# Order of the first key and value products in a two-way cross attention: the next sequence's keys placed before this sequence's values

## The chip, the cores and the metric

The kernel runs on one core of one Trainium2 chip. Its time is device microseconds for one execution. The five engines are named as the profile names them: PE (matmul; PEld its weight loads), DVE (vector), ACT (scalar), POOL (GpSimd) and SP (which issues most DMAs). All data are float32.

## The reference, cut to what matters

There are 16 sequences of 100 rows of `x` (640 wide), each with an encoder context of 722 rows (384 wide). The last 4 context rows are the tokens. Eight heads of 80.

```python
query = hidden_states @ Wq
keyt = enc @ Wk          # 718 keys
valt = enc @ Wv
hs = _mha(query, keyt, valt)
ca_q1 = jnp.einsum('btc,th->bch', ca, Wq_ca)[:, indices, :]
ca_hs1 = _mha(ca_q1, residual, residual)
ca_q2 = ca_hs1 @ Wq
ca_hs2 = _mha(ca_q2, ca @ Wk_ca, ca @ Wv_ca)
out = (hs + ca_hs2) @ Wout + b_out + residual
```

## The kernel before, in words

One loop `for b in range(B)` goes over the sequences, and from there on the order in which the program is written is the order of each engine's queue; each engine works through its own queue in that order and waits only on semaphores.

The middle sequences, b = 1 to 14, run like this:

- *Scores.* `scores` (products L609) fills PSUM with the scores of sequence b in three groups. Groups 0 and 2 lie in two double banks from the pool `pair`; group 1 lies in two banks of the pool `psumk` and two of `psum1`. ACT copies them to `st` (L665 for the double banks, L659 for the others). DVE takes the maximum over them (`most`, L1270 and L1282).
- *Tokens' product.* `now.softmax2()` (L1287) multiplies the exponentials `e1` with the tokens' table `y_sb` on PE: 64 small matmuls (L825) into `z_ps`, one bank of `psum1`. DVE reads it (L834, L836).
- *Keys of b + 1 and values of b.* Both are 3 by 2 blocks of products of the context with a weight. They are done with 15 products instead of 18, by sums of context pieces and of weights made before (a fast scheme for small matrix products). POOL makes the sums of the context, 13 additions (`enc_sums`, L500), one sequence ahead; other pieces are used as loaded. The plans `V_PLAN` and `K_PLAN` list the 15 products in order, each with the bank it is summed in (A to E) and the block that the running sum goes to. `go(n)` of a `Values` or `Keys` object takes the next n products: the matmuls (V: L434, two of them, one per half of the keys; keys: L465, two), and behind each the transfer of the running sum: for a block's first arrival a copy on ACT (L407, into `vs` or `kT`), for a later one an addition on DVE (L405). A bank's next product must wait until the running sum has been read. `both(n)` takes n of V's and then n of the keys'.
- *Banks.* V's A and B are a pair of double banks, which held the scores of group 2. V's C, D and E take two banks of `psum1` each. The keys' A and B are the two banks of `psumk`, which held scores of group 1; their C, D and E are one bank of `psum1` each.
- *Softmax.* While these products run, DVE and ACT turn the maximum into `top.over` (`top.go`, L700 to L730; ACT's part is `spread`, L722), DVE subtracts it from `st` (L1258), and ACT takes exponentials (L1266).
- *POOL* works through the next sequence's first token scores (`scores1`, L798 and L805; its first instruction waits for the maximum over this sequence's scores), small pieces of the second softmax (L864, L878), the bias on rows of `x` (L932, only in sequences that load such rows), and the tokens' values (`values2`, L892, L899).
- After the products come the fifth chunk of the next keys (`last_keys`, L559), in some sequences the output projection (L1050) and the next queries (L535), and then the attention's sum `a_ps` (L1455).

The order around the change: `softmax2` (L1287), `second.scores1` (POOL, L1345), `top.go(3)` (DVE, L1346), `both(3)` (L1347), `scores2` (L1348).

Of the kernel before, what the change touches and what calls it, by code (L numbers as in the profile page):

```python
# [126 lines left out]
def kernel(  # L127
# [80 lines left out]
    def enc_tile(name):  # L208

        return inp.tile([P, NF, KT], F32, tag="enc", name=name)  # L210
# [14 lines left out]
    def load_rest(b, enc):  # L225
        if b == 1:
            room = hsT_tile("rest_1").rearrange("p c s -> p (c s)")
            rest = room[:, : len(A_REST) * KT].rearrange("p (i k) -> p i k", k=KT)
        else:
            rest = rest_tile(f"rest_{b}")  # L230
        for (u, c), i in A_REST.items():
            nc.sync.dma_start(
                out=rest[:, i], in_=enct[b][:, c, u * (KT - 1) : u * (KT - 1) + KT]
            )
        return enc[0], rest
# [348 lines left out]
    def last_keys(b, enc):  # L584
        banks = pair(f"kT_ps_{b}")
        return chunk_keys(
            HC - 1,
            [banks[:, k] for k in range(2)],
            [wk4[:, c] for c in range(CC)],
            enc,  # L590
        )
# [140 lines left out]
    def load_m(b):  # L732
        if b < 2:
            return lambda c: m_sb[c][:, b * HT : (b + 1) * HT]
        mb = small.tile([P, HC, HT], F32, tag="mb", name=f"mb_{b}", bufs=2)
        nc.sync.dma_start(
            out=mb, in_=m_d[:, :, b * HT : (b + 1) * HT].rearrange("c p n -> p c n")
        )
        return lambda c: mb[:, c]
# [496 lines left out]
    for b in range(B):  # L1236
# [5 lines left out]
        def loads():  # L1242

            if b == 0:
                nc.sync.dma_start(
                    out=wout_sb, in_=wout.rearrange("(c p) n -> p c n", p=P)
                )
            if b + 2 >= B:
                return None, None
            x_next = xT_at[0] if b % 2 else load_x(p + 1)  # L1250
            xT_at[0] = x_next
            return Second(b + 2, x_next), load_enc(b + 2)
# [4 lines left out]
        def subtract(i):  # L1257
            return nc.vector.tensor_tensor(  # L1258
                st[i],
                st[i],  # L1260
                top.over[:KN].unsqueeze(1).to_broadcast([KN, 2, ROWS]),
                ALU.subtract,
            )

        def exponential(i):
            nc.scalar.activation(st[i], st[i], AF.Exp, scale=SCALE)  # L1266
# [26 lines left out]
        if b + 1 < B:  # L1293
            kk = Keys(b + 1, enc)
# [32 lines left out]
        elif b + 1 < B:  # L1327
            vv = Values(b, e_in)

            def both(n):  # L1330
                vv.go(n)
                kk.go(n)

            forms = [wout_sb[:, 2 * i : 2 * i + 2, k * (H // 2) : (k + 1) * (H // 2)]
                     for i in range(2) for k in range(2)]
            if b == 2:
                for o, left, right in (
                    (forms[1], forms[1], forms[0]),
                    (wout2[:, 0], forms[3], forms[1]),
                    (wout2[:, 1], forms[2], wout2[:, 0]),  # L1340
                ):
                    nc.gpsimd.tensor_tensor(o, left, right, ALU.subtract)
            elif last.b - 1 in PAIRS:
                nc.gpsimd.tensor_tensor(wout2[:, 0], wout2[:, 0], forms[0], ALU.add)
            second.scores1(seen, range(T - 1))  # L1345
            top.go(3)  # L1346
            both(3)  # L1347
            now.scores2(nc.gpsimd)  # L1348
            second.scores1(None, range(T - 1, T))
            if b == 1:  # L1350
                now.load()
            last.load()
            top.go(1)
            if b > 1:
                last.place()
            now.exponentials2()
            both(2)
            both(2)
            top.go()
            both(1)  # L1360
            now.softmax3()
            if b == 1:
                nc.gpsimd.tensor_tensor(last.hs[:S], last.hs[:S], last.hs2, ALU.add)
            if last.b in PAIRS:
                last.sums()
            now.values2()
            vv.go(2)
            kk.go(1)
            subtract(0)
            exponential(0)  # L1370
            vv.go(1)
            subtract(1)
            vv.go(1)
            kk.go(2)
            exponential(1)
            vv.go(1)
            kk.go(2)
            both(1)
            both(1)
            if b == 1:  # L1380
                for f in list(wv_there):
                    nc.scalar.copy(wv_sb[:, W_AT[f]], wv_there.pop(f))
            second.load()
            if b == 1:
                nc.gpsimd.dma_start(out=bias, in_=bout[0].partition_broadcast(P))
            second_next, enc_next = loads()
            if b + 2 < B:
                m_next = load_m(b + 2)
            subtract(2)
            exponential(2)  # L1390
            last_keys(b + 1, enc)
            if b + 2 < B:
                enc_next = load_rest(b + 2, enc_next)
            if b == 1:
                last.transpose()
            if last.b in PAIRS:
                second.softmax1(3)
                last.project_pair()
                if last.b == max(PAIRS):
                    nc.sync.dma_start(  # L1400
                        out=forms[1],
                        in_=wout[: 2 * P, H // 2 :].rearrange("(c p) n -> p c n", p=P),
                    )
            second.softmax1()
        else:
            room = enc_tile("spare").rearrange("p f k -> p (f k)")
            spare.extend(room[:, i * H : (i + 1) * H] for i in range(2))
            last.transpose()
            vv = Values(b, e_in)
            last.load()  # L1410
            mine.load()
            top.go(3)
            vv.go(3)
            last.project_few(len(OC) - 2)
            now.scores2(nc.gpsimd)
            now.exponentials2()
            top.go(1)
            vv.go(2)
            top.go()
            vv.go(3)  # L1420
            now.softmax3()
            now.values2()
            vv.go(2)
            subtract(0)
            exponential(0)
            vv.go(5)
            for i in (1, 2):
                subtract(i)
                exponential(i)
            last.project()  # L1430
# [108 lines left out]
```

## Time and profile before

| what | time |
|---|---|
| median of 3 runs | 927.17 us (927.08 to 928.4) |
| the profiled execution | 927.45 us, span 925.7 us |
| PE busy | 916.2 us, 99% of the span |
| POOL, DVE busy | 684.5 us, 680.8 us (74% each) |
| ACT busy | 433.6 us (47%) |
| V's products into A (L434) | 352 matmul rows of 437 ns |
| keys' products into A (L465) | 360 matmul rows of 367 ns |
| waits of PE for ACT at V's first product | 2.6 us, 9 times |

A row of a timeline gives start and length in us (starts from the beginning of the span), engine, line, operation, tile written <- tiles read, shapes and count of instructions merged into it; in brackets stands how long the engine sat idle before it and what ended that. The matmuls are pipelined, so the rows of consecutive groups overlap by a few tenths; the distance between the starts of two groups is the better measure of what a group costs. A row of waits reads: engine, tile and line that waited, <- engine, tile and line it waited for: us in total, times, longest. A row of the chain of waits gives shares of the span.

### The profile page before, as it was taken

The page shows a single profiled execution, that of the slowest core. Times are in us where ns is not written, and L with a number is a line of the kernel's source. Part 1 is how long each engine was busy: PE and PEld are TensorE (multiplying, and loading weights), DVE is VectorE, ACT ScalarE, POOL GpSimd, SP SyncE. Part 2 cuts the span into 40 slices and gives each one's busy share as a digit, 9 for nine tenths or more (in the row PEclk, how much of TensorE's full clock was granted, in tenths as well). Part 3 has the DMA queues.
Part 4 walks back from the last instruction along what each step waited for, and adds up shares of the span by engine and source line. Part 5 has one row for each costly group of instructions (what it writes and reads, how often), then busy time and mean ns, then how long its engine had stood idle before and what let it go on. Part 6 is the DMA issues. An engine that isn't in the chain of part 4 may idle for free.

```text
span 925.7 us, 26204 instructions
## 1 busy us (share of the span) xinstructions
PE 916.2 (99%) x11290; PEld 772.5 (83%) x11290; DVE 680.8 (74%) x1085; ACT 433.6 (47%) x836; POOL 684.5 (74%) x647
## 2 busy tenths in 40 slices
PE   9999999999999999999999999999999999999998
PEld 6988889787797979888798787988879787797866
DVE  3459795989739896785967869579883898838883
ACT  2235543737336463552636426264641737427341
POOL 5749999787937878497884968757996579956723
PEclk9999999999999999999999999999999999999999
DMA  8822023050300304031030411205031050310201
GB/s 263 273 76 78 25 60 83 5 152 2 107 27 17 112 6 127 3 98 58 23 111 3 110 46 30 76 2 154 3 91 42 2 154 2 104 45 2 82 19 41
DMA packets 49675, 62.85 MB, mean 68 GB/s; under 512 B 14072, under 2 KB 38200, under 8 KB 49560
## 3 DMA queue, kind: packets, MB, share of 16 engines
q1 hardware_dynamic: 45512, 51.49, 18.6%
q0 software_dynamic: 3024, 8.53, 3.1%
q8 instruction: 89, 1.46, 0.7%
q10 hardware_dynamic: 1024, 1.15, 0.4%
q14 instruction: 26, 0.21, 0.1%
HBM read 55.59 MB, written 5.57 MB: 66 GB/s over the span
## 4 chain that ended last, share of the span: by engine, by line
PE 97%; ACT 1%; DMA 0%; issue 0%; DVE 0%; POOL 0%; ACTq 0%; POOLq 0%
PE s_ps L609 12%; PE a_ps L1455 12%; PE v_psA L434 11%; PE v_psB L434 9%; PE k_psA L465 8%; PE kT_ps L559 8%; PE q_ps L535 7%; PE k_psB L465 7%; PE o_ps L1050 5%; PE v_psC L434 3%; PE k_psC L465 3%; PE v_ps L375 2%; PE v_psD L434 2%; PE v_psE L434 2%; PE y_ps L773 1%; PE k_psE L465 1%
## 5 line engine op out<-in xcount | busy, mean ns | idle before, releaser
L798 POOL TENSOR_TENSOR e<-ca,g 100x800 f32<-100x800 f32 x64 | 97.9, 1540 | 124.7 <-PE v_psD L434 99.8
L500 POOL TENSOR_TENSOR enc<-enc 128x240 f32<-128x240 f32 x135 | 109.8, 822 | 18.3 <-DMA enc<-in_enct 11.2
L1258 DVE TENSOR_TENSOR st<-st,over 120x1600 f32<-120x1600 f32 x48 | 117.4, 2448 | 0.0
L1455 PEld LDWEIGHTS a_ps<-vs,st 120*36 120x36 f32 (+3 forms) x3072 | 109.2, 125 | 4.9 <-issue 4.8
L434 PE MATMUL v_psA<-wv_sb,enc 128*120 128x320 f32 x352 | 110.6, 437 | 2.5 <-ACT st L665 2.3
L1455 PE MATMUL a_ps<-vs,st 120*36 120x81 f32 (+3 forms) x3072 | 112.0, 233 | 0.0
L899 POOL TENSOR_TENSOR hs<-hs,hs 100x640 f32<-100x640 f32 x48 | 99.0, 2063 | 3.8
L805 POOL TENSOR_TENSOR e<-e,e 100x800 f32<-100x800 f32 x48 | 93.6, 1950 | 3.8
L892 POOL TENSOR_TENSOR hs<-vb,p 100x640 f32<-100x640 f32 x64 | 91.3, 1436 | 3.9 <-DMA vb<-va_d 0.9
L434 PE MATMUL v_psB<-wv_sb,enc 128*120 128x320 f32 x296 | 91.9, 433 | 0.0
L1266 ACT ACTIVATE st<-st 120x1600 f32<-120x1600 f32 x48 | 73.9, 1539 | 33.4 <-DVE st L1258 33.4
L465 PE MATMUL k_psA<-enc,wk_sb 128*128 128x240 f32 x360 | 87.7, 367 | 0.0
L434 PEld LDWEIGHTS v_psA<-wv_sb,enc 128*120 128x120 f32 x352 | 63.2, 183 | 26.5 <-ACT st L665 3.8
L465 PEld LDWEIGHTS k_psA<-enc,wk_sb 128*128 128x128 f32 x360 | 68.4, 190 | 16.7
L1270 DVE TENSOR_TENSOR most<-most,st 120x800 f32<-120x800 f32 x64 | 67.6, 1056 | 15.8 <-ACT st L659 14.7
L609 PE MATMUL s_ps<-qp,kT 64*56 64x100 f32 (+1 forms) x3072 | 73.6, 248 | 0.1
L465 PE MATMUL k_psB<-enc,wk_sb 128*128 128x240 f32 x300 | 73.0, 366 | 0.0
L434 PEld LDWEIGHTS v_psB<-wv_sb,enc 128*120 128x120 f32 x296 | 54.2, 183 | 21.8 <-DVE vs L405 0.4
L609 PEld LDWEIGHTS s_ps<-qp,kT 64*56 64x56 f32 (+1 forms) x3072 | 67.1, 130 | 5.7 <-issue 4.5
L965 ACT COPY hsT<-turned_hs 32x160 f32<-32x160 f32 (+7 forms) x244 | 67.7, 278 | 3.0
L535 PE MATMUL q_ps<-xT,wq_sb 128*128 128x200 f32 x400 | 69.1, 333 | 0.0
L535 PEld LDWEIGHTS q_ps<-xT,wq_sb 128*128 128x128 f32 x400 | 67.8, 190 | 1.0 <-issue 0.5
(168 smaller groups left out, 1766.2 us busy)
## 6 DMA issues: line engine op xcount, KB each, us to landing
vb<-va_d POOLq DMA_DIRECT2D x32, 250.0 KB, 3.8
vb<-va_d SPq DMA_DIRECT2D x32, 250.0 KB
enc<-in_enct SPq DMA_DIRECT2D x30, 240.0 KB
enc<-in_enct SPq DMA_DIRECT2D x15, 360.0 KB
xT<-in_xt SPq DMA_DIRECT2D x8, 500.0 KB
rest<-in_enct SPq DMA_DIRECT2D x31, 120.0 KB
xn<-in_x SPq DMA_DIRECT2D x11, 320.0 KB
out<-xn SPq DMA_DIRECT2D x11, 320.0 KB
```

The lines of the kernel that those rows point to most:

```text
L434: nc.tensor.matmul(at[0][j][:KN, : H // 2], a_form(self.enc, f)[:, j * KN : (j + 1) * KN], wv_there.get(f, wv_sb[:, W_AT[f]]), start=first ...
L465: nc.tensor.matmul(at[:, i * KT : (i + 1) * KT], wk_sb[:, W_AT[f], i], a_form(self.enc, f), start=(first and i == 0), stop=last, skip_grou ...
L500: nc.gpsimd.tensor_tensor(out, left, right, op)
L535: nc.tensor.matmul(q_ps[:, : 2 * S].rearrange("p (j s) -> p j s", j=2), wq_sb[:, c, n * P : (n + 1) * P], xT[:, :, c, :], start=(c == 0), ...
L559: nc.tensor.matmul(bank[:, i * KT : (i + 1) * KT], weights[c], a_raw(enc, u, c), start=(i == 0 and c == 0), stop=(c == CC - 1), skip_group ...
L609: nc.tensor.matmul(s_ps[at][k0:k1, cols], w, rhs, start=not begun & {(at, k) for k in range(k0, k1, 32)}, stop=last, skip_group_check=True,)
L798: first = nc.gpsimd.tensor_tensor(to, self.ca[:, t, :].unsqueeze(1).to_broadcast([S, NH, S]), g[:, :, t].unsqueeze(2).to_broadcast([S, NH, ...
L805: nc.gpsimd.tensor_tensor(e, e, to, ALU.add)
L892: first = nc.gpsimd.tensor_tensor(to, self.vb[t][:S].rearrange("p (h d) -> p h d", h=NH), p2[:, :, t].unsqueeze(2).to_broadcast([S, NH, D] ...
L899: nc.gpsimd.tensor_tensor(sums, sums, to, ALU.add)
L1258: return nc.vector.tensor_tensor(st[i], st[i], top.over[:KN].unsqueeze(1).to_broadcast([KN, 2, ROWS]), ALU.subtract,)
L1455: nc.tensor.matmul(a_v[lo:hi, h % 4], st[i // 2][: KEYS[i], i % 2, h * S + lo : h * S + hi], block(i, h // 4)[: KEYS[i], h % 4], start=(i ...
```

## The change

In the middle sequences `both(3)` is taken apart: the keys' three products for sequence b + 1 are issued first, directly behind the tokens' product, and V's three for sequence b behind them. Before, V's three came first. The same instructions are issued. On PE six matmuls change places with six, on ACT three copies into `kT` with four into `vs`. The queues of DVE, POOL and SP are as before. As the banks of `psum1` are handed out in turn, they now fall like this: the keys' D takes the bank that V's first D half had (a score bank of group 1), V's first D half takes the bank of `z_ps`, which V's second half had, and V's second D half takes the keys' D bank once ACT has copied it.

```diff
@@ -1344,7 +1344,8 @@
                 nc.gpsimd.tensor_tensor(wout2[:, 0], wout2[:, 0], forms[0], ALU.add)
             second.scores1(seen, range(T - 1))
             top.go(3)
-            both(3)
+            kk.go(3)
+            vv.go(3)
             now.scores2(nc.gpsimd)
             second.scores1(None, range(T - 1, T))
             if b == 1:
```

## The prediction

> **What bounds the kernel now.** I read the page first (share of each engine, then the chain that ended last), then the waits of the tensor engine, then the timeline of one sequence. The page:
>
> ```profile
> span 925.7 us, 26204 instructions
> PE 916.2 (99%) x11290; PEld 772.5 (83%) x11290; DVE 680.8 (74%) x1085; ACT 433.6 (47%) x836; POOL 684.5 (74%) x647
> PE 97%; ACT 1%; DMA 0%; issue 0%; DVE 0%; POOL 0%; ACTq 0%; POOLq 0%
> ```
>
> PE is busy 916.2 of 925.7 us and is 97% of the chain. The change removes no work, so all it can gain lies in the moments when PE stands still. The waits of PE, and two rows of the waits of all engines:
>
> ```profile
> PE v_psA L434 <- ACT st L665: 2.6, 9, 0.3
> ...
> PEld k_psC L465 <- DVE vs L405: 0.5, 2, 0.3
> ```
>
> The longest is the very place that the change touches: the first V product of a sequence waits for ACT's copy of the last score banks (L665), 9 times, 2.6 us in all. The second row, V's and the keys' later meeting with DVE, will matter below. Here is the place in sequence 6, all engines in order of start:
>
> ```profile
> 380.86 0.75 PE L825 MATMUL z_ps<-y_sb,e 100*32 100x33 f32 x64
> 381.02 1.55 ACT L665 COPY st<-s_ps 120x800 f32<-120x800 f32 x2 [0.91 <-PE s_ps L609]
> 381.90 1.34 PE L434 MATMUL v_psA<-wv_sb,enc 128*120 128x320 f32 x4 [0.29 <-ACT st L665]
> 383.07 1.24 PE L434 MATMUL v_psB<-wv_sb,enc 128*120 128x320 f32 x4
> 383.27 0.69 ACT L407 COPY vs<-v_psA 120x640 f32<-120x640 f32 x1 [0.70 <-PE v_psA L434]
> 384.94 0.91 ACT L407 COPY vs<-v_psD 120x320 f32<-120x320 f32 x2
> 385.23 0.97 PE L465 MATMUL k_psA<-enc,wk_sb 128*128 128x240 f32 x4
> 386.04 0.97 PE L465 MATMUL k_psB<-enc,wk_sb 128*128 128x240 f32 x4
> 386.24 0.56 ACT L407 COPY kT<-k_psA 128x480 f32<-128x480 f32 x1 [0.39 <-PE k_psA L465]
> 387.66 1.24 PE L434 MATMUL v_psA<-wv_sb,enc 128*120 128x320 f32 x4
> 388.31 1.73 ACT L722 COPY spread<-mx 64x800 f32<-64x800 f32 x2
> ```
>
> The tokens' product (z_ps) ends at 381.61. V's bank A is one of the pair that held the last scores, so PE stands until ACT's first copy is out (copies start at 381.02, 1.55 for two) and goes on at 381.90. The key products three places later need none of these banks.
>
> **The change, part by part.** In the 14 sequences 1 to 14 the six matmuls of the keys' first three products go ahead of V's six. Nothing is added or removed; POOL, SP and DVE keep their order; on ACT the three copies into kT now stand ahead of the four into vs.
>
> *What z leaves PE without the wait.* Where no wait follows z, the next product starts 0.68 us after z does; sequence 0 (y_ps, then k_psA) and 15 (a transpose) show it:
>
> ```profile
> 67.32 0.75 PE L825 MATMUL z_ps<-y_sb,e 100*32 100x33 f32 x64
> 68.00 0.96 PE L773 MATMUL y_ps<-m,xT 128*64 128x72 f32 x20
> 68.89 1.08 PE L465 MATMUL k_psA<-enc,wk_sb 128*128 128x240 f32 x4
> ...
> 882.49 0.75 PE L825 MATMUL z_ps<-y_sb,e 100*32 100x33 f32 x64
> 883.17 0.65 PE L977 MATMUL hst_ps<-ident,hs_sb 100*128 100x100 f32 x5
> ```
>
> In sequence 6 it is 381.90 - 380.86 = 1.04. So a whole wait is worth 1.04 - 0.68 = 0.36 us (at least the 0.29 that PE counts as idle). The first product after the switch is about 0.1 longer (v_psA 1.34 against 1.24, k_psA 1.08 against 0.97): whoever comes first pays it, so this stays.
>
> *Five sequences have less to gain.* z itself is late in 2, 3, 4, 7 and 9, from gaps that the profile calls issue, and part of ACT's copy already lies under that:
>
> ```profile
> 162.83 1.04 PE L825 MATMUL z_ps<-y_sb,e 100*32 100x33 f32 x64
> 163.87 0.53 PE L434 MATMUL v_psA<-wv_sb,enc 128*120 128x320 f32 x1
> ...
> 211.05 0.95 PE L825 MATMUL z_ps<-y_sb,e 100*32 100x33 f32 x64
> ...
> 277.84 0.27 PE L825 MATMUL z_ps<-y_sb,e 100*4 100x33 f32 x9 [0.25 <-issue]
> 278.03 1.34 PE L434 MATMUL v_psA<-wv_sb,enc 128*120 128x320 f32 x4
> ...
> 438.26 0.97 PE L825 MATMUL z_ps<-y_sb,e 100*32 100x33 f32 x64
> ...
> 551.82 0.98 PE L825 MATMUL z_ps<-y_sb,e 100*32 100x33 f32 x64
> ```
>
> z of 1.04 is 0.29 longer than 0.75 and leaves 0.07; 0.95 leaves 0.16; in sequence 4 the product follows z's end (277.84 + 0.27 = 278.11) without a gap and nothing is left; 0.97 and 0.98 leave 0.14 and 0.13. Together 0.5 us. The program up to z is the same, so I keep these gaps where they are.
>
> *New order of copies and banks.* Reckoned for sequence 6, with the groups' pitches from the rows (V 1.08, keys 0.81, 0.92 for the first): k_psA starts at 381.54, V's A at 384.08, ready at about 385.36, copied by 386.05. PE comes back to A at 387.3 (now 387.66), 1.25 us later; before, that slack was larger by the three key groups. The copies of bank D end at about 388.0, where before the last key copy ended at 388.42, so ACT's spread (L722, 388.31) is not later. The keys' bank D must now be copied (about 384.9) before V's second D product at 386.8: slack 1.9. Both are covered; if ACT came more than 1.25 late, PE would stand for the rest.
>
> *The keys' data earlier by 3.7 us.* k_psA reads the first of POOL's thirteen sums (L500) for the next sequence. The tightest is sequence 1, where V's first product starts at 106.92 now and the sums run late:
>
> ```profile
> 101.76 0.69 POOL L500 TENSOR_TENSOR enc<-enc 128x240 f32<-128x240 f32 x1
> ```
>
> It ends at 102.45, and k_psA would start at about 106.56: 4 us to spare. No cost.
>
> *Where the lead is lost again.* PE leads by 0.36 only if what it meets next is released by PE itself. DVE's work after the third V product waits for PE, so it moves along. But POOL's row of work is released by DVE's maximum over the scores, which the change does not move, and in some sequences POOL holds DVE up. Sequence 11 (DVE, with one row of 13; POOL; PE), and then sequence 6:
>
> ```profile
> 673.32 4.09 DVE L1258 TENSOR_TENSOR st<-st,over 120x1600 f32<-120x1600 f32 x1
> 677.34 0.88 DVE L405 TENSOR_TENSOR vs<-v_psC,vs 120x320 f32<-120x320 f32 x2
> ...
> 787.02 4.15 DVE L1258 TENSOR_TENSOR st<-st,over 120x1600 f32<-120x1600 f32 x1
> ```
>
> ```profile
> 660.48 3.04 POOL L798 TENSOR_TENSOR e<-ca,g 100x800 f32<-100x800 f32 x2 [1.08 <-DVE most L1270]
> 672.69 3.05 POOL L932 TENSOR_TENSOR xn<-xn,bias 128x640 f32<-128x640 f32 x2
> 675.69 1.82 POOL L878 TENSOR_TENSOR p<-e,sm 100x32 f32<-100x32 f32 x1
> ```
>
> ```profile
> 677.87 1.08 PE L465 MATMUL k_psC<-enc,wk_sb 128*128 128x240 f32 x4
> ```
>
> ```profile
> 398.50 1.81 DVE L1258 TENSOR_TENSOR st<-st,over 120x1600 f32<-120x1600 f32 x1
> 400.79 1.03 DVE L405 TENSOR_TENSOR vs<-v_psC,vs 120x320 f32<-120x320 f32 x2 [0.48 <-PE v_psC L434]
> ```
>
> The first subtraction takes 1.81 in sequence 6, 4.09 in 11 and 4.15 in 13. In 11 it starts inside POOL's two bias additions (672.69 to 675.74); it ends at 677.41, one undisturbed length behind them. The addition of v_psC behind it frees the bank that k_psC takes, and k_psC already starts late (its group is 1.08, the length after a stop). This end hangs on POOL, so in sequence 11, and in 13, the other of the two waits in the row of k_psC above, PE arrives 0.36 earlier and waits 0.36 longer: gain 0. In sequence 6 the addition itself waits 0.48 for PE, so there is room.
>
> [...]
>
> **The sum.** Nine whole waits less the two (11, 13): 7 x 0.36 = 2.5; the five with a late z 0.5; in all 3.0 us. The profiled execution took 927.45 us (span 925.7); the median of the runs is 927.17, 0.28 below. 927.17 - 3.0 = 924.2. Bounds of the gain: 7 x 0.29 = 2.0 with nothing from the five; 2 x 0.36 less again if POOL's lateness in 11 and 13 also grows with the lead of the sequence before, 1.3; above, 9 x 0.36 + 0.5 = 3.7, and 14 x 0.36 = 5.0 if the late z were gone too.
>
> **The rivals.** *All whole waits are kept (chance 0.10).* DVE's subtraction in 11 and 13 comes early enough to go between POOL's additions, or ahead of them. Speaks for it: 0.36 is of the size by which such a race is decided. Against: it would start at 672.96, still behind 672.69. Time 927.17 - 3.7 = 923.5.
>
> *The gain is given back (0.13): no change.* Somewhere in each sequence PE meets a release that hangs on the scores, not on itself, with less than 0.36 us to spare, as in 11 and 13. For it: DVE is 74% and POOL 74% busy. Against: in the waits, only the two of k_psC are of this kind; in sequence 6 the DVE addition there waits for PE. Time about 927.0.
>
> *ACT's copies stop PE (0.09): slower.* V's A bank is refilled 3.2 us after its first product instead of 5.8, with three key copies ahead in ACT's queue. If its copy came 1.25 + 0.36 = 1.6 us later than reckoned, the sequence would lose; at 2.0 late each of 14 loses 0.4, 5.5 in all: 932.7. For it: ACT is strictly in order in the rows. Against: ACT waits for PE before these copies (0.70, 0.39 in the rows), so it has no backlog.
>
> **How the numbers follow.** My forecast, 924.2 with its own range 923.2 to 925.9 (gains 4.0 to 1.3), has 0.65; the three rivals 0.10, 0.13 and 0.09; 0.03 is left for other ways, shared out. The range over the cases runs from 922.7, inside the case without late z, to 927.1, which takes in the given-back gain. A difference under 0.2% (1.85 us) can't be told from none here. Faster: 0.65 x 0.94 + 0.10 + 0.01 = 0.72; same: 0.13 + 0.04 + 0.01 = 0.18; slower 0.10.
>
> **What would show it.** In the changed profile: k_psA starts 0.68 us after an undisturbed z; the wait of v_psA for st L665 is gone from PE's waits, and PE's busy time stays while its span shrinks by about 3 us. v_psA's second group starts without a wait for vs L407. The waits of k_psC for DVE vs L405 grow from 0.5 to about 1.2 us, in sequences 11 and 13. The five late z stay late. I am wrong if the span between two sequences' z shrinks by less than 0.3 in 1, 5, 6, 8, 10, 12 and 14; if PE waits for ACT's vs copies; or if k_psC waits in more than those two.

## The result and the profile after

| | before | changed |
|---|---|---|
| median (range) | 927.11 us (926.66 to 928.4) | 924.5 us (923.55 to 926.3) |
| profiled execution, span | 927.45 us, 925.7 us | 925.05 us, 923.3 us |
| from z of sequence 2 to z of sequence 15 | 719.66 us | 716.48 us |

The ratio is 0.9973, with a 95% interval from 0.9963 to 0.9983: 2.6 us faster, more than the 0.2% (1.85 us) that the prediction took as the least that can be told. The page of the changed kernel (span, busy shares, chain):

```profile
span 923.3 us, 26190 instructions
...
PE 916.2 (99%) x11290; PEld 772.4 (84%) x11290; DVE 679.9 (74%) x1085; ACT 434.2 (47%) x836; POOL 682.1 (74%) x647
...
PE 96%; DVE 3%; DMA 1%; issue 0%; POOL 0%; ACTq 0%; DVEq 0%; POOLq 0%
```

PE is busy for the same 916.2 us, and the span is 2.4 shorter. ACT's 1% of the chain is gone, and DVE has 3% where it had none; such a share is a stretch of the path, not a loss. The waits of PE and its weight loads name the change (engine, tile and line <- what it waited for: us in total, times, longest):

```profile
PE k_psC L465 <- DVE vs L405: 0.4, 2, 0.2
...
PEld k_psC L465 <- DVE vs L405: 1.3, 3, 0.6
```

The row that was longest before, v_psA for st L665, does not occur any more. What has grown is k_psC's wait for DVE: 0.5 before, 1.3 now. The place of the change in sequence 6 (the timeline; start, length, engine, line, operation, tiles):

```profile
380.52 0.75 PE L825 MATMUL z_ps<-y_sb,e 100*32 100x33 f32 x64
380.68 1.55 ACT L665 COPY st<-s_ps 120x800 f32<-120x800 f32 x2 [0.91 <-PE s_ps L609]
381.20 1.08 PE L465 MATMUL k_psA<-enc,wk_sb 128*128 128x240 f32 x4
...
383.74 1.24 PE L434 MATMUL v_psA<-wv_sb,enc 128*120 128x320 f32 x4
...
385.01 0.69 ACT L407 COPY vs<-v_psA 120x640 f32<-120x640 f32 x1 [0.52 <-PE v_psA L434]
...
386.97 1.24 PE L434 MATMUL v_psA<-wv_sb,enc 128*120 128x320 f32 x4
```

The key product starts 0.68 after z, without a wait, while ACT still copies the scores until 382.23. V's first product is 1.24 long, the length without a stop before it (1.34 with one, in the kernel before). Its bank is out at 385.01 + 0.69 = 385.70, and PE comes back to it at 386.97.

The steadiest ruler in these traces is the stretch between the z of sequence 2 and that of sequence 15, 13 sequences:

```profile
163.59 0.81 PE L825 MATMUL z_ps<-y_sb,e 100*32 100x33 f32 x64
...
880.07 0.75 PE L825 MATMUL z_ps<-y_sb,e 100*32 100x33 f32 x64
```

880.07 - 163.59 = 716.48, against 882.49 - 162.83 = 719.66 before: 3.2 us less. Sequence 1, ahead of the ruler, is 0.7 shorter. The spans differ by only 2.4, since the changed kernel's execution was slower ahead of all this: its first z came at 68.8 instead of 67.3. That start is not the change's: the same kernel, run again, had its first z at 67.4 (last section).

### The profile page after: what moved, and what is told of

Its sections match the earlier page's. It is cut to its first block, busy times and chain, and to the rows that moved or that the text cites. A ratio compares the mean times of both kernels' runs of the same rounds, so it can differ in the third digit from the quotient of the medians.

```text
span 923.3 us, 26190 instructions
## 1 busy us (share of the span) xinstructions
PE 916.2 (99%) x11290; PEld 772.4 (84%) x11290; DVE 679.9 (74%) x1085; ACT 434.2 (47%) x836; POOL 682.1 (74%) x647
## 4 chain that ended last, share of the span: by engine, by line
PE 96%; DVE 3%; DMA 1%; issue 0%; POOL 0%; ACTq 0%; DVEq 0%; POOLq 0%
PE a_ps L1456 12%; PE s_ps L609 12%; PE v_psA L434 10%; PE v_psB L434 8%; PE kT_ps L559 8%; PE k_psA L465 8%; PE q_ps L535 7%; PE k_psB L465 6%; PE o_ps L1050 5%; PE v_psC L434 3%; PE k_psC L465 3%; PE v_ps L375 2%; PE v_psD L434 2%; PE v_psE L434 2%; PE y_ps L773 1%; PE k_psD L465 1%
## 5 line engine op out<-in xcount | busy, mean ns | idle before, releaser
L805 POOL TENSOR_TENSOR e<-e,e 100x800 f32<-100x800 f32 x48 | 93.6, 1950 | 3.8
L892 POOL TENSOR_TENSOR hs<-vb,p 100x640 f32<-100x640 f32 x64 | 88.0, 1386 | 5.9 <-DMA vb<-va_d 3.0
L609 PE MATMUL s_ps<-qp,kT 64*56 64x100 f32 (+1 forms) x3072 | 73.5, 248 | 0.0
L609 PEld LDWEIGHTS s_ps<-qp,kT 64*56 64x56 f32 (+1 forms) x3072 | 67.1, 130 | 5.5 <-issue 4.2
```

The costliest lines, as they stand in the source:

```text
L609: nc.tensor.matmul(s_ps[at][k0:k1, cols], w, rhs, start=not begun & {(at, k) for k in range(k0, k1, 32)}, stop=last, skip_group_check=True,)
L805: nc.gpsimd.tensor_tensor(e, e, to, ALU.add)
L892: first = nc.gpsimd.tensor_tensor(to, self.vb[t][:S].rearrange("p (h d) -> p h d", h=NH), p2[:, :, t].unsqueeze(2).to_broadcast([S, NH, D] ...
```

## The experiments

The theory: at z, ACT's copy of the last scores (1.55 us, ending about 1.7 after z starts) held V's first bank, and any 0.4 us of other work placed there hides it; part of that lead is lost in sequences 11 and 13, where k_psC waits for a DVE subtraction that two POOL additions hold up. Besides the time, each run is judged by the ruler of 13 sequences (before 719.66, changed 716.48), which leaves the start out. The table splits the ruler at V's first E product, the first into bank E (`v_psE`): the place of the change lies before it, k_psC's waits behind it. The scores' end is the end of the last score product (L609) ahead of z.

| sequences 2 to 14, summed, us | before | changed | changed again | load later | load earlier | key ahead of z | eight copies |
|---|---|---|---|---|---|---|---|
| scores' end to V's first E product | 136.57 | 132.88 | 132.87 | 133.20 | 132.76 | 134.49 | 142.85 |
| from there to the next scores' end | 583.09 | 583.59 | 583.99 | 583.42 | 583.06 | 584.24 | 582.60 |

The kernel before ran beside all of them: median 927.03 beside the load earlier, the changed kernel again and the ACT copies, 927.02 beside the others. The changed kernel ran only beside the former.

### One key product ahead instead of three

The edit as against the changed kernel:

```diff
-            kk.go(3)
+            kk.go(1)
             vv.go(3)
+            kk.go(2)
```

> Only the keys' first product (0.92 us on the tensor engine) goes ahead of V's three; the keys' second and third follow V's. Theory (what counts is only that at least 0.36 us of other work covers the rest of the score copy): as the changed kernel, 924.5 us, no wait of v_psA for st L665. Rival (three products are needed, or the gain comes from another effect of the order, such as the banks or the order of ACT's copies): between 925.5 and 927.1 us.

Measured: 923.48 us (922.73 to 926.25), ratio 0.9967 [0.9954, 0.9979]; ruler 716.60, the same as with three. PE in sequence 6:

```profile
381.56 0.75 PE L825 MATMUL z_ps<-y_sb,e 100*32 100x33 f32 x64
382.24 1.08 PE L465 MATMUL k_psA<-enc,wk_sb 128*128 128x240 f32 x4
383.15 1.24 PE L434 MATMUL v_psA<-wv_sb,enc 128*120 128x320 f32 x4
```

V's first product comes 1.59 after z's start and does not wait: the profile has no wait of v_psA for st L665. One product (0.91) is all the cover that is needed; the other two bring nothing more. That three are needed is refuted. The banks of `psum1` are handed out here in the same order as in the kernel before, so the gain does not come from that either. The profiled execution, one of the slower ones (925.62), lost 1.9 us once, in sequence 1 (last section).

### The bias load later, in the changed kernel and in the one before

POOL's bias additions (L932) belong to `last.load()`. It is moved behind the subtraction that they hold up:

```diff
-            last.load()
             top.go(1)
...
             now.softmax3()
+            last.load()
```

> The changed kernel with the bias additions on rows of x (last.load) moved on GpSimd behind the small product of softmax3, so that they no longer stand ahead of the first subtraction. Theory (in sequences 11 and 13 the lead is lost because the subtraction waits for these additions): the three waits of k_psC for DVE vs L405 (1.3 us at the weight loads) vanish, first subtraction 1.8 us in all sequences, 923.5 to 923.8 us. Rival (the lateness moves to the next subtraction and the same wait comes one product later): 924.5 us, waits of about 1 us at another product.

> The kernel before with the same move of the bias additions as in the run on the changed kernel. Theory (without the lead, the collision of subtraction and bias additions costs only the two short waits of k_psC, 0.5 us at the weight loads): 926.6 to 927.1 us, so the move is worth 0.1 to 0.5 us here and 0.7 to 1.0 us on the changed kernel. Rival (the move has a worth of its own): the same gain on both.

Measured, changed kernel: 923.23 us (922.3 to 924.96), ratio 0.9957 [0.9945, 0.997]; ruler 716.61. Kernel before: 927.1 us, ratio 1.0 [0.9991, 1.0009]; ruler 720.03. In the changed kernel k_psC's wait is gone. The DVE's subtractions of sequence 11, and POOL's bias additions, show where it went:

```profile
670.30 1.77 DVE L1258 TENSOR_TENSOR st<-st,over 120x1600 f32<-120x1600 f32 x1
...
673.35 4.20 DVE L1258 TENSOR_TENSOR st<-st,over 120x1600 f32<-120x1600 f32 x1
```

```profile
672.13 3.05 POOL L932 TENSOR_TENSOR xn<-xn,bias 128x640 f32<-128x640 f32 x2
```

```profile
PEld v_psB L434 <- DVE vs L405: 1.8, 6, 0.4
```

The first subtraction now takes its undisturbed 1.77, but the additions hold up the second one (4.20, ending at 677.55, 2.4 behind them), and the last row shows PE waiting for DVE one product later. One of its six waits, 0.36 us in sequence 15, is in the kernel before too; the other five, 1.4 us in sequences 3, 6, 8, 11 and 13, stand in place of k_psC's 1.3 in three. So the additions do cause k_psC's wait, and taking them from this place moves most of the lateness: behind V's first E product the sequences together take 0.2 us less than in the changed kernel's first execution and 0.6 less than in its second, and its late z, longer in sum, take 0.3 of that back. The ruler shows nothing. The rival's mechanism came, though the median, 923.23, lies below both expected times; the changed kernel did not run beside it. In the kernel before, where PE has no lead to lose there, the move is worth nothing either: PE still waits for ACT at z,

```profile
PE v_psA L434 <- ACT st L665: 3.2, 11, 0.3
```

and the order of V and keys, not the load, makes the difference between 720 and 716.5.

### The bias load earlier

```diff
             now.scores2(nc.gpsimd)
+            last.load()
             second.scores1(None, range(T - 1, T))
...
-            last.load()
             top.go(1)
```

> The changed kernel with the bias additions (last.load) ahead of the last pair of token scores on GpSimd. Then the pair L798, L805, of which the second needs the first, stands where the two bias additions stood when the first subtraction starts. Theory (the vector engine gets in wherever GpSimd leaves a gap, 0.08 us between L798 and L805 in sequence 1 of the profile before, and not between two additions that follow without one): the first subtraction ends by 20.5 us behind the scores in all sequences, the k_psC waits vanish, the second subtraction isn't blocked by bias additions either, 923.2 to 923.7 us. Rival (any GpSimd work holds the subtraction up to the end of the row): the same waits of k_psC, 924.5 us, or more.

Measured: 923.11 us (921.93 to 924.52), ratio 0.996 [0.9947, 0.9972]; ruler 715.82, the shortest of all, 0.7 and 1.0 below the changed kernel's two executions. Of k_psC's waits for DVE only one of 0.2 us at a weight load is left, in sequence 1, and behind V's first E product the sequences take 583.06, as little as the kernel before (583.09), where PE had no lead to lose. DVE's first subtraction in sequence 11, then POOL around it:

```profile
672.00 2.38 DVE L1258 TENSOR_TENSOR st<-st,over 120x1600 f32<-120x1600 f32 x1
```

```profile
669.65 1.55 POOL L932 TENSOR_TENSOR xn<-xn,bias 128x640 f32<-128x640 f32 x1
671.16 1.54 POOL L798 TENSOR_TENSOR e<-ca,g 100x800 f32<-100x800 f32 x1
672.78 3.35 POOL L805 TENSOR_TENSOR e<-e,e 100x800 f32<-100x800 f32 x1
```

The subtraction starts during POOL's multiplication (671.16 to 672.70). POOL's next instruction reads that result and starts 0.08 later, and DVE gets in ahead of it: it waits 0.7 and then runs 1.7, ending at 674.38, while POOL's addition takes 3.35 instead of its undisturbed 1.88. Not all of the expectation held: in sequences 1 and 3 the first subtraction ends 22.8 and 21.3 us behind z's start, not by 20.5; in 3 it starts during POOL's addition L805, and PE loses nothing by it. This version has the shortest steady stretch. By time alone it can't be told from the changed kernel run beside it (924.01, next but one): their ranges overlap.

### One key product ahead of z

If the late starts of z come from what stands just ahead of it, large products there instead of scores should remove them.

```diff
         st.append(scores(b, 2, tiles))
+        if 0 < b < B - 1:
+            kk = Keys(b + 1, enc)
+            kk.go(1)
         now.softmax2()
...
-            kk.go(3)
+            kk.go(2)
             vv.go(3)
```

> The changed kernel with the keys' first product put between the scores and the tokens' product. Theory (the late starts within z come from the supply of instructions after the dense scores, and are now on the path where the score copy covered them before): the key product of 0.92 us, with four matmuls, lets the supply catch up; the late z vanish (1.0 us in the profile of the changed kernel), 923.5 us with less spread between runs. Rival 1 (the gaps have another cause): 924.5 us, gaps of the same size. Rival 2 (the vector engine reads z 0.9 us later and its maximum with it, so GpSimd and the subtraction are later): waits of k_psC grow, 924.5 to 926 us.

Measured: 925.86 us (924.87 to 927.61), ratio 0.9985 [0.9976, 0.9994]; ruler 717.72. In this run the ruler flatters: z of sequence 2 has a key product ahead of it and starts 1.0 later behind the scores, while z of sequence 15 has none. From scores' end to scores' end the same 13 sequences take 718.73, which is 1.9 to 2.3 more than the changed kernel. PE in sequence 6:

```profile
381.28 1.08 PE L465 MATMUL k_psA<-enc,wk_sb 128*128 128x240 f32 x4
382.28 0.75 PE L825 MATMUL z_ps<-y_sb,e 100*32 100x33 f32 x64
382.96 1.08 PE L465 MATMUL k_psB<-enc,wk_sb 128*128 128x240 f32 x4
```

No z of the 14 is late any more: each is 0.75 long, and from the end of the scores to V's first E product every sequence but one takes 10.34 (sequence 2: 10.38). But that is longer than the changed kernel's mean of 10.22, which has its late z in it. There are now two places where a key product comes first after another form of tile, and each group there is 1.08 instead of 0.97 (k_psA and k_psB above); z itself starts 1.00 after k_psA, 0.08 more than the 0.92 between k_psA and the next key product. Two new rows of waits appear as well, and a third has grown:

```profile
PEld z_ps L825 <- ACT st L665: 4.3, 14, 0.3
PEld k_psA L465 <- issue: 3.2, 13, 0.2
...
PEld k_psC L465 <- DVE vs L405: 1.8, 5, 0.6
```

They are of the weight loads, which overlap PE's other work (770.6 us of them beside 918.9 of products, in a span of 925.8), so their sums are no cost by themselves. But k_psC's wait, 1.3 in three before, is now 1.8 in five, sequence 8 among them, as the second rival said, and behind V's first E product the sequences take 0.65 and 0.25 more than in the changed kernel's two executions; that the later reading of z is the cause is not shown. The late starts depend on what precedes z, as supposed; the time expected from removing them was wrong, because the key product ahead of z costs 0.20 in every sequence (10.34 against 10.14; the 0.11 of the longer group and the 0.08 ahead of z make up nearly all of it), and the late starts only 0.08 on average (10.22 against 10.14).

### The changed kernel again

> The changed kernel once more, beside the run with the bias additions moved ahead of the last token scores. 924.0 to 924.6 us, waits of k_psC for DVE vs L405 near 1.3 us at the weight loads. If the late starts within z belong to an execution and not to the program, they stand in other sequences than 2, 4, 5 and 7 and sum to about 1 us again; if to the program, in the same sequences with the same lengths.

Measured: 924.01 us (922.6 to 925.88), ratio 0.9969 [0.9958, 0.998]; ruler 716.86. k_psC's wait is again 1.3 us. The z of the same sequence in two executions of one program (columns: stretch, its length, busy time and count of PE, of PEld, of DVE, clock, DMA share, GB/s; only z's instructions are counted), first as above:

```profile
208.00:216.00 8.00, 0.75 (x64) 0.64 (x64) 0.62 (x2) 1.00 0.02 4
...
435.00:443.00 8.00, 0.94 (x64) 0.71 (x64) 0.63 (x2) 1.00 0.02 4
```

and here:

```profile
208.00:216.00 8.00, 0.92 (x64) 0.72 (x64) 0.62 (x2) 1.00 0.01 4
...
435.00:443.00 8.00, 0.78 (x64) 0.67 (x64) 0.63 (x2) 1.00 0.01 2
```

In sequence 3 z is undisturbed in the one and late in the other, in sequence 7 nearly the reverse. So the program alone does not fix which z is late. It is not free either: sequences 2, 4 and 5 are late in both executions, the sum is 1.0 us in both, and in all ten profiled executions no z outside sequences 2 to 9 is late. The expectation's two cases were too simple.

### ACT late: four and eight copies between the keys and V

To measure by how much ACT may be late before PE waits for V's bank A, idle copies of a scratch tile are put into ACT's queue; nothing that is computed depends on them.

```diff
             kk.go(3)
+            for _ in range(4):  # and 8
+                nc.scalar.copy(idle, idle)
             vv.go(3)
```

> The changed kernel with four small extra copies on the scalar engine (about 1.1 us in all) between the keys' three copies and V's. Theory (V's bank A has 1.25 us of slack between its copy and its next product): no wait of v_psA for ACT vs L407, 924.3 to 924.9 us. Rival (the copies are nearer to the path than reckoned): waits of V's second group in most sequences, 927 us or more.

> The same with eight extra copies (about 2.2 us). Theory: V's second product into A waits about 0.9 us for ACT vs L407 in each of 14 sequences, 935 to 938 us. Rival (the slack is larger, or the extra copies run in idle time of the scalar engine ahead of V's copies): 924.5 to 927 us.

Measured with four: 925.42 us (923.19 to 926.66), ratio 0.9979 [0.997, 0.9988]; ruler 716.24, no wait of v_psA for vs L407. The median is above what was expected, but not because of the copies in the middle sequences: the profiled execution lost 2.4 us once, in sequence 0 (k_psA waited 1.4 for a DVE addition into kT), and the times fall into two groups, 923.2 to 925.0 and 925.9 to 926.7.

With eight: 932.99 us, one execution; ruler 725.45, 9.0 more than the changed kernel. PE waits in all 14 sequences; ACT and then PE in sequence 6, where z starts at 383.03:

```profile
PE v_psA L434 <- ACT vs L407: 7.2, 14, 0.5
```

```profile
386.90 2.61 ACT L1349 COPY idle<-idle 128x128 f32<-128x128 f32 x8
389.41 0.69 ACT L407 COPY vs<-v_psA 120x640 f32<-120x640 f32 x1
```

```profile
386.24 1.24 PE L434 MATMUL v_psA<-wv_sb,enc 128*120 128x320 f32 x4
...
390.15 1.07 PE L434 MATMUL v_psA<-wv_sb,enc 128*120 128x320 f32 x3 [0.52 <-ACT vs L407]
```

Copy A now ends 7.07 after z's start instead of 5.18: it is 1.89 late. (One record of the second v_psA group is missing.) PE starts 0.05 behind the copy's end, 7.12 after z instead of 6.45: 0.67 late. So the first 1.22 of the lateness cost nothing. From the scores to V's first E product a sequence takes 10.92 instead of 10.14, which is 0.78: the 0.67 and about 0.1 for the longer first product after a stop (1.34 against 1.24 in the kernel before). Summed over the 13 sequences that is 10.0 more (table), late z included, and behind V's first E product they take 1.0 less, mainly because k_psC's wait no longer occurs: together the ruler's 9.0. The expectation of 935 to 938 was too high: of the 2.61 us of idle copies, 0.52 fall into the time in which ACT waited for PE anyway, and 0.2 lies under the overlap of its instructions, 0.10 at each end of the idle copies.

## Why the prediction was right

924.2 was forecast and 924.5 measured. The mechanism is the one foretold: ACT's copy is covered at z, and the lead is lost again in sequences 11 and 13. By its steps:

- *The whole wait, 0.36.* As foretold: after an undisturbed z the next product starts at 0.68 instead of 1.04, and the wait for st L665 is gone. From the scores' end to V's first E product an undisturbed sequence takes 10.14 instead of 10.50.
- *"Five sequences have less to gain."* The size came out roughly, by luck in part; the places did not. "The five late z stay late" in 2, 3, 4, 7 and 9 was wrong: in the changed kernel's first execution they are in 2, 4, 5 and 7, in the second in 2, 3, 4 and 5, and by 0.03 us in 7. The step's premise, "the program up to z is the same, so I keep these gaps where they are", fails, because the same program does not repeat them. Their sum is 1.0 us in each, where it was 1.4 before. Before, ACT's copy had covered them: all sequences but one took 10.50, late z or not. With the cover gone they count in full: the mean is now 10.22, not 10.14. The gain at z is 4.0 in the fourteen sequences (0.29 each on average), where the prediction had 9 x 0.36 + 0.5 = 3.7.
- *The new order of copies and banks.* All three times held: V's A starts 3.22 after z, is copied at 5.18, and is needed again at 6.45. The slack of 1.25 was measured as 1.22 by the eight idle copies, and four fit into it. The rival in which ACT's copies stop PE falls: it needed copies 1.6 later than reckoned, and they came on time.
- *The keys' data earlier.* No wait of the keys for POOL's sums appeared in the changed kernel.
- *Where the lead is lost.* 1.2 us of waits of k_psC were foretold and 1.3 came: 0.56 and 0.55 at the weight loads in 11 and 13, as named, and 0.19 in sequence 3. From z to z sequences 11 and 13 gained 0.03 and 0.09, and in the second execution nothing, as foretold. Sequence 3 lost 0.09 of its gain: in the kernel before, the subtraction is held up there and in 8 as well (3.80 and 3.61), which the prediction does not list. DVE, POOL and PE in sequence 11 of the changed kernel:

```profile
671.48 4.32 DVE L1258 TENSOR_TENSOR st<-st,over 120x1600 f32<-120x1600 f32 x1
675.72 0.88 DVE L405 TENSOR_TENSOR vs<-v_psC,vs 120x320 f32<-120x320 f32 x2
```

```profile
671.08 3.04 POOL L932 TENSOR_TENSOR xn<-xn,bias 128x640 f32<-128x640 f32 x2
674.07 1.83 POOL L878 TENSOR_TENSOR p<-e,sm 100x32 f32<-100x32 f32 x1
```

```profile
676.26 1.08 PE L465 MATMUL k_psC<-enc,wk_sb 128*128 128x240 f32 x4 [0.19 <-DVE vs L405]
```

The subtraction starts 0.40 behind the first addition and ends at 675.80, 1.68 behind the second: nearly all of its own 1.77 lies after both. No semaphore holds the subtraction: its row shows no wait, only a length of 4.32. So, against the description of the kernel before, an engine here waits on more than semaphores. By the rows the two engines take turns in this place: L878, behind both additions in POOL's queue, takes 1.83 where it took 0.24 in sequence 6 of the kernel before, and ends at 675.90, 0.10 behind the subtraction. What decides which of them goes first the trace does not tell. In 11 and 13 the rival that all whole waits are kept falls. Not foretold: in sequence 6 the subtraction is held up too. POOL and DVE there, before:

```profile
397.09 4.63 POOL L932 TENSOR_TENSOR xn<-xn,bias 128x640 f32<-128x640 f32 x2
...
398.50 1.81 DVE L1258 TENSOR_TENSOR st<-st,over 120x1600 f32<-120x1600 f32 x1
```

and changed:

```profile
396.74 3.05 POOL L932 TENSOR_TENSOR xn<-xn,bias 128x640 f32<-128x640 f32 x2
...
397.81 3.66 DVE L1258 TENSOR_TENSOR st<-st,over 120x1600 f32<-120x1600 f32 x1
```

Before, the subtraction started 0.13 ahead of the first addition's end (398.63) and ran right behind it, and the second addition had to wait (4.63 for the two). PE's lead brings it 0.34 further into the first addition, and there it is passed by the second. k_psC does not wait in sequence 6, since the addition behind the subtraction had 0.48 to spare.
- *The sum.* In the 13 sequences of the ruler, 3.7 gained at z less 0.5 lost behind it (0.33 in 11, 0.26 in 13, the rest nearly cancels) is 3.2; in the second execution 3.7 less 0.9 is 2.8. With sequence 1, which gains 0.35 at z, that is 3.5 and 3.2, a little above the 3.0 predicted. The medians show 2.6, with an interval of 1.6 to 3.4 (0.9983 to 0.9963). The median also holds one-time losses of the early sequences that have no part in the sum (last section), so that 924.2 and 924.5 lie so close is in part luck.
- *The signs of being wrong.* Two of them appeared, small. k_psC waits in a third place in the first execution, sequence 3, though not in the second. And from z to z sequences 5 and 10 shrank by 0.19 and 0.28 in the first execution, and 5 by 0.15 in the second, less than the 0.3 set as the least; in 5 the reason is its late z, which the prediction kept elsewhere. Neither touches the mechanism.

The rival that the gain is given back in every sequence is excluded by 14 k_psA without a wait and a ruler that is 3.2 and 2.8 shorter.

## What to carry to other kernels

When a bank must be copied out before PE may reuse it, look for one product that uses another bank and put it there: 0.9 us of it hid the whole 0.36 us wait, and two more added nothing. A wait that is removed uncovers what it had hidden (here late starts of about 1.0 us in all), and an engine that runs ahead meets the next release that does not hang on it, so a gain per sequence is counted only up to that place. Where the gain is a few tenths per period, compare a long steady stretch within the trace that begins and ends at the same point of the program: here the first z alone moved between 66.9 and 68.8 us, and one-time losses took 1.8 to 2.4 us more, against a change worth 3.

## What was not expected of the hardware

*The start varies between executions.* The first products (L375) run at about half pace for some microseconds. In the profiled executions, two matmuls of one form took 1.27 us at 7.65 in the changed kernel, but 0.70 at 7.44 in the kernel before, and 0.74 already at 4.75 in the changed kernel with its load later (changed, before, load later):

```profile
7.65 1.27 PE L375 MATMUL v_ps<-wv_sb,rest 128*120 128x320 f32 x2
```

```profile
7.44 0.70 PE L375 MATMUL v_ps<-wv_sb,rest 128*120 128x320 f32 x2
```

```profile
4.75 0.74 PE L375 MATMUL v_ps<-wv_sb,enc 128*120 128x320 f32 x2
```

The granted clock from 4 to 8 us reads 1.00 in the first two, and the third has a mean of 1.0 over its execution, so the profile's clock does not show it. The first z came at 68.8 us in the first of these and at 67.3 in the second. The moment at which the pace changes moved by more than 2.9 us between executions, from before 4.75 to after 7.65; what sets it no run here shows.

*One-time losses.* Some executions lose 1.8 to 2.4 us once in sequence 0 or 1 (sequence 1 with one key product ahead and with the load early, sequence 0 with four ACT copies). In sequence 1 the profile names the wait (one key product ahead):

```profile
PE v_psC L434 <- ACT vs L407: 1.3, 1, 1.3
```

That copy stands in ACT's queue behind an activation (L870) that waited 9.9 us for a product on POOL (L864), and in both runs POOL reached that product about 2 us later behind z than in the changed kernel. What made POOL late was not followed further. The times of the kernel before lie mostly between 926.3 and 927.7, with a few up to 929.6, while those of the changed kernel are spread over 922.6 to 926.3; that such losses and the start make up this spread is likely from the profiled executions, but not shown for the others, and why the changed order should meet them more often was not settled.

*A waiting DVE subtraction and POOL.* The first subtraction was passed by the second of two bias additions that follow each other without a gap in all five sequences of the changed kernel that have them (3.66 to 4.33 us for a subtraction of 1.77), and in four of the five in the kernel before (3.61 to 4.15); in sequence 6 there it went between them. With the load early it got in where POOL's next instruction reads the result of the one that runs and starts 0.08 us behind it (2.38). The lack of a gap is not the whole condition: the small product L878 follows the second addition just as closely and is itself held up (in sequence 11 it starts at 674.07, where the additions end at 674.12, and takes 1.83). What decides which of the two goes first, also in sequence 6, is open.

*Late starts of z.* They make a z, 64 small matmuls behind the scores, up to 0.65 us longer. They are not in the same sequences in each execution, but in all ten executions they lie in sequences 2 to 9; sequence 2 is late in each of the nine without a product ahead of z, by 0.03 to 0.65. None of 14 is late behind four large ones. That they come from the supply of instructions, as the word issue suggests, is only argued.
